# A graph transformer kernel: the last rows of x loaded first, six raw chunks in place of four at the start of layer 2, and three last chunks scaled one by one

## The chip, the cores and the metric

The kernel runs on one core of a Trainium2 chip, all in fp32. The time is the device time of one execution in microseconds (us), as the median of several runs. A profiled execution gives, beside its own time, the span from its first to its last instruction and a trace of every instruction.

## The reference

Two transformer convolutions over one graph, N = 6250 nodes with D = 128 features, E = 106,250 edges sorted by `dst`, H = 2 heads of C = 64; a batch norm and a relu between them; at the end the residual with x and a layer norm.

```python
def conv(h, edge_attr, src, dst, Wq, bq, Wk, bk, Wv, bv, We, Ws, bs):
    q, k, v = heads(h @ Wq + bq), heads(h @ Wk + bk), heads(h @ Wv + bv)
    e = heads(edge_attr @ We)                       # 96 attributes of an edge
    alpha = einsum('ehc,ehc->eh', q[dst], k[src] + e) / sqrt(C)
    ex = exp(alpha - segment_max(alpha, dst)[dst])
    a = ex / segment_sum(ex, dst)[dst]
    return segment_sum((v[src] + e) * a[:, :, None], dst) + h @ Ws + bs

edge_attr = concatenate([cos((node_vec[src] - t)[:, None] * time_w + time_b), msg])
h = conv(x, edge_attr, src, dst, ...)               # layer 1
h = relu((h - h.mean(0)) / sqrt(h.var(0) + 1e-5) * bn_g + bn_b)
h = conv(h, edge_attr, src, dst, ...)               # layer 2
return layernorm(x + h)
```

## The kernel before

**Tiles.** The edges are cut into NC = 106 chunks. A chunk has up to CE = 1024 edges (eight row tiles of 128) that end in up to NN = 64 nodes, 64 x 2 heads = 128 columns. Because `Wq` and `Wk` are multiplied together ahead of time, a node's query is a column of a *table*: `tables` makes 512 nodes' worth of it (a *block*, 13 of them) and writes it to DRAM, and a chunk loads its 64 nodes from there.

**A layer** is a call of `conv` (L699): one loop over rounds k (L964), in an order written out by hand (`manual_schedule`), so every engine gets its instructions in the order of the code. In round k:
- `fetch` and `gather` bring in chunk k+2 (layer 2) or k+4 (layer 1). `fetch` has SP issue the loads of the edge attributes, the table and, in layer 2, the stored time encoding, transposed attributes and residual. `gather` (L746) issues eight indirect DMAs on GpSimd, one per row tile of 128 source nodes. Each is made to wait for a step of TensorE (`behind`), so that the gathers of one chunk are spread over a round.
- TensorE scores chunk k (`score`, L840 and L841, in two halves), transposes the weights of chunk k-1 (`turn_weights`, L863), turns chunk k+1 (`turn_in`, L819), finishes chunk k-2 (`finish_turn`, `finish`), and sums the weighted rows of chunk k-1 (`gather_sums`, L871). The last sum's step releases the first gather of the next round.
- VectorE takes the minimum of the scores (`lowest`), divides the sums of chunk k-2 (`divide`, L878 to L881) and copies them for `finish` (L896). ScalarE takes the exponential (`weigh`, L853) and copies the turned tiles out of PSUM.
- `pull(extra, n)` (L1019) takes n steps of other work from a generator, `rest()`.

**What the layers read.** Layer 1 gathers from `xv_d`, a copy of x in DRAM with each node's time ahead of its row. At the start, SP loads x in four cuts of 12 row blocks (`load_features`, L502), then the last 106 rows that fill no whole block (`pl.rest`). `pass_features` (L520) copies the cuts beside the times, on VectorE and ScalarE in turns, and SP writes each to `xv_d`, the rest rows first of all. The code at L1338 to L1347 sets the order of these copies against the first table's matmuls and additions (`first_table`), and of `columns(flats[0], srcs)`, which makes the gathers' indices.

Layer 1 leaves its result h in SBUF, transposed (`hT`), 64 nodes per chunk; SP's DMA puts each there (L910). Layer 1's `rest()` (L1081) turns finished blocks of h back to rows and writes them to `h_d` in DRAM, each once `at_round[0]` has passed the last chunk that it needs by three; two of the blocks are left to round NC+1. At the end of layer 1 the batch norm's scale and shift are known, and layer 2 wants relu(scale*h + shift). The normalised rows go to a second array, `hn_d`, 13 blocks: `hide(n)` (L769) turns and writes n blocks (tile `fhn`, four buffers; VectorE's copy is L1065, SP's writes L1073 and L1078). Three are written in the run-up of layer 2, the others in rounds 0 and 1. Until they are there, chunks 0 to RAW-1 gather from `h_d`, raw; ScalarE then normalises the turned copy as it leaves PSUM (L821) and VectorE the rows themselves, for the sums (`normalise`, L886 and L887, three operations over 128x1024). Later chunks gather from `hn_d` and need neither.

Layer 2's `rest()` (L1175) makes block b of the table and of the residual x + h Ws in seven pulls, then two idle ones; a chunk can't be fetched before its block is written.

**The end.** `finish` of layer 2 collects centred rows in groups of up to ten chunks, which begin at the chunks in `STARTS` (L59). When a group's last chunk is in, ScalarE takes one square root for the group (L940), VectorE its reciprocal (L941), and each chunk's rows wait in `done` for `store` (L945): ScalarE scales them, SP writes them to the output. The last chunk's store is made up of two chunks' rows (`flast`, L954). All stores go through SP's queue.

Of the kernel before, what the change touches and what calls it, by code (L numbers as in the profile page):

```python
# [13 lines left out]
P = 128  # L14
# [33 lines left out]
NC = 106  # L48
# [7 lines left out]
HIGHEST = 2.0 ** 119  # L56

LG = 10
STARTS = (*range(0, 91, LG), 97, 102, 105)  # L59


@with_exitstack
# [439 lines left out]
def load_features(nc, pl, mw, x, node_vec):  # L502

    N = x.shape[0]
    NF = N // P
    NR = N - NF * P
    xall = pl.xall = pl.hT[:, :NF * D].rearrange("p (b d) -> p b d", d=D)
    pl.cuts = list(zip(range(0, NF, 12), [*range(12, NF, 12), NF]))
    for b0, b1 in pl.cuts:
        nc.sync.dma_start(xall[:, b0:b1], x[:NF * P, :].rearrange("(p b) d -> p b d", b=NF)[:, b0:b1])  # L510
        if b0 == 0:
            pl.times = mw.tile([P, NF], F32, name="fnv", bufs=1)
            nc.sync.dma_start(pl.times, node_vec[:NF * P].rearrange("(p b) -> p b", b=NF))
    if NR:
        nc.vector.memset(pl.rest, 0.0)
        nc.sync.dma_start(pl.rest[:NR, 1:], x[NF * P:N, :])
        nc.sync.dma_start(pl.rest[:NR, 0:1], node_vec[NF * P:N].rearrange("(p a) -> p a", a=1))


def pass_features(nc, pl, mw, dram, N):  # L520

    NF = pl.xall.shape[1]
    pl.xv_d = dram.tile([N, 1 + D], F32, name="xv_d")
    rows = mw.tile([P, NF, 1 + D], F32, name="fxrows", bufs=1)
    nc.vector.tensor_copy(rows[:, :, 0], pl.times)
    to = pl.xv_d[:NF * P, :].rearrange("(p b) d -> p b d", b=NF)
    if N > NF * P:
        nc.sync.dma_start(pl.xv_d[NF * P:N, :], pl.rest[:N - NF * P])
    for i, (b0, b1) in enumerate(pl.cuts):
        (nc.scalar.copy if i % 2 else nc.vector.tensor_copy)(rows[:, b0:b1, 1:], pl.xall[:, b0:b1])  # L530
        nc.sync.dma_start(to[:, b0:b1], rows[:, b0:b1])
        yield

# [127 lines left out]
def ordered(ctx: ExitStack, tc: tile.TileContext, pl, x, dst, edge_attr_64, conv2, bn_g, bn_b, out):  # L661


    nc = tc.nc
    N = x.shape[0]
# [9 lines left out]
    at_round = [0]  # L675
# [16 lines left out]

    SINGLE = 40

    RAW = 4

    hidden = list(range(-(-N // GE)))

    def conv(c, extra, first_blocks=None):  # L699
# [46 lines left out]
        def gather(k, rows, behind=None):  # L746
            f = ch[k].f
            for t in rows:
                row = nc.gpsimd.indirect_dma_start(  # L749
                    out=f[:, t, (1 if c else 0):1 + D], out_offset=None, in_=(h_d[:N, :] if k < RAW else hn_d) if c else pl.xv_d,  # L750
                    in_offset=bass.IndirectOffsetOnAxis(ap=pl.srcs[:, t, k:k + 1], axis=0))
# [6 lines left out]
        def lead(k):  # L758
            return 2 if c else AHEAD
# [9 lines left out]
        def hide(n):  # L769
            step = None  # L770
            for b0 in hidden[:n]:
                step = put_rows(hn_d, b0, *turned_rows(b0, small.tile([P, GE // P, P], F32, name="fhn", bufs=4)))
            del hidden[:n]
            return step
# [35 lines left out]
        def turn_in(k, u):  # L810
# [7 lines left out]
            for t in range(4):  # L818
                last = nc.tensor.transpose(px[:, t * P:(t + 1) * P], s.f[:, u * 4 + t, 1:1 + D], ident)  # L819
            if c and k < RAW:  # L820
                nc.scalar.activation(s.ft[:, u * GE:(u + 1) * GE], px, AF.Relu, bias=pl.shift, scale=pl.scale)  # L821
# [12 lines left out]
        def score(k, u):  # L834

            s = ch[k]
            if u == 0:
                s.ps = p_s.tile([P, CE], F32, name="fps")
            w = slice(u * GE, (u + 1) * GE)
            half = nc.tensor.matmul(s.ps[:, w], s.tab[:, :, 0], s.ft[:, w], start=True, stop=False)  # L840
            return half, nc.tensor.matmul(s.ps[:, w], s.tab[:EC, :, 1], s.et[:, w], start=False, stop=True)  # L841
# [33 lines left out]
        def divide(k):  # L875
            s = ch[k]
            inv = small.tile([P, 1], F32, name="finv")
            nc.vector.tensor_scalar(inv, s.pa[:, D + ED:], 1e-30, None, op0=OP.max)  # L878
            nc.vector.reciprocal(inv, inv)
            s.a = small.tile([P, D + EW], F32, name="fa")  # L880
            nc.vector.tensor_scalar(s.a, s.pa, inv, None, op0=OP.mult)  # L881
# [16 lines left out]
        def finish(k):  # L898
# [24 lines left out]

            k0 = max(i for i in STARTS if i <= k)
            g = k - k0
            n = next(i for i in (*STARTS, NC) if i > k) - k0
            if g == 0:
# [30 lines left out]
        def pull(gen, n):  # L958
            for _ in range(n):
                next(gen, None)  # L960

        with cs, tc.manual_schedule():
            ended = None
            for k in range(-lead(-NC), NC + 3):  # L964
                def on(j):
                    return 0 <= j < NC

                coming = [j for j in range(k + lead(k - 1), k + lead(k) + 1) if on(j)]
                filling = False

                def bring(rows, behind=None):
                    for j in coming:
                        gather(j, rows, behind)

                for j in coming:
                    fetch(j)
                if k == -lead(-NC):
                    yield_first(bring)
                elif k < -1:
                    bring(range(T))  # L980
                elif not filling:
                    bring(range(1), ended)
                step = score(k, 0)[1] if on(k) else hide(1) if c and k == -1 else None
                if k >= -1 and not filling:
                    bring((1,), step)
                step = turn_weights(k - 1) if on(k - 1) else hide(1) if c and k == -1 else None
                if k >= -1 and not filling:
                    bring((2,), step)
                place()
                if on(k - 2):  # L990
                    divide(k - 2)
                half, step = score(k, 1) if on(k) else (hide(1) if c and k == -1 else None, None)
                if k >= -1 and not filling:
                    bring((3,), half if c else step or half)
                    if c:
                        bring((4,), step)
                if on(k - 2):
                    finish_turn(k - 2)
                if on(k):
                    lowest(k)  # L1000
                step = turn_in(k + 1, 0) if on(k + 1) else None
                if k >= -1 and not c:
                    bring(range(5) if filling else (4,), step)
                if on(k):
                    weigh(k)
                step = turn_in(k + 1, 1) if on(k + 1) else None
                if k >= -1:
                    bring((5,), step)
                for j in (k + 2,) if k < SINGLE else (k + 2, k + 3) if k == SINGLE else (k + 3,):
                    if c == 0 and on(j):  # L1010
                        encode(j)
                        if j < SINGLE + 3:
                            sine()
                if k >= 0:
                    at_round[0] = k
                    if c and k < 2:
                        hide(5)
                    else:
                        pull(extra, 2 if k < 4 or k > 96 else 1)  # L1019
                if len(args) == 3 or args and k == NC - 4:  # L1020
                    sine()
                if on(k - 2):
                    finish(k - 2)
                if c and on(k):
                    if k < RAW:
                        normalise(k)
                    nc.vector.tensor_copy(ch[k].f[:, :, 1 + D:1 + D + TD], ch[k].z)
                for _ in range(min(len(done), 4 if k >= NC else 2 if k > NC - 12 else 1)):
                    store(*done.pop(0))
                *steps, ended = gather_sums(k - 1) if on(k - 1) else (None, None, None)  # L1030
                if k >= -1:
                    for t, step in zip((6, 7), steps):
                        bring((t,), step)
            at_round[0] = 2 * NC
            for _ in extra:
                pass
            for rows in done:
                store(*rows)
# [4 lines left out]
    with tc.tile_pool(name="fpw", bufs=2) as pw:  # L1043
# [131 lines left out]
        def rest():  # L1175
            for b0 in range(1, NT):
                yield from block(b0)
                yield
                yield

        conv(1, rest(), first_blocks)


@with_exitstack
def tile_gnn_resnorm(ctx: ExitStack, tc: tile.TileContext, x, src, dst, edge_attr_64, edge_weight, node_vec,
                     time_w, time_b, conv1, conv2, bn_g, bn_b, out):
    nc = tc.nc
    N = x.shape[0]
# [10 lines left out]
    with tc.tile_pool(name="plan", bufs=1) as pl, tc.tile_pool(name="planw", bufs=2) as mw, \  # L1199
# [66 lines left out]
        NR = -(-NC // 16) * 16  # L1266
# [39 lines left out]
        passed = pass_features(nc, got, mw, made, N)  # L1306
# [32 lines left out]
        first_table = tables(nc, got, 0, xT0, 0, mw, wide)  # L1339
        next(first_table)  # L1340
        next(first_table)
        next(passed)
        for _ in first_table:
            pass
        columns(flats[0], srcs)
        for _ in passed:
            pass  # L1347
        got.tw = broadcast(nc, keep, "ftw", time_w, TD)
        got.tb = broadcast(nc, keep, "ftb", time_b, TD)
        nc.sync.dma_start(got.wv[0], conv1["Wv"])  # L1350
# [55 lines left out]
```

## Time and profile before

| | us |
|---|---|
| median of three runs | 2306.39 (2305.79 to 2308.45) |
| the profiled execution | 2306.31 |
| its span | 2304.3 |
| start to the first gather of layer 1 | 39.25 |
| from there to the first gather of layer 2 | to 1184.96 |
| the last gather of layer 2 | 2267.0 |

The mean granted clock of TensorE in the profiled execution is 0.983 of full speed. Busy time by stretch of the span (us from its start):

| stretch | TensorE | VectorE | ScalarE | GpSimd | granted clock | DMA engines' mean busy share |
|---|---|---|---|---|---|---|
| 0 to 39 | 22.9 | 20.1 | 9.9 | 5.0 | 0.87 | 0.84 |
| 40 to 1178, layer 1 | 1119.1 | 786.3 | 733.4 | 816.9 | 0.99 | 0.62 |
| 1178 to 1256, change of layer | 58.3 | 38.9 | 30.2 | 46.1 | 0.87 | 0.79 |
| 1256 to 2268, layer 2 | 988.5 | 386.7 | 440.6 | 759.9 | 0.99 | 0.67 |
| 2268 to 2304 | 22.3 | 10.7 | 13.1 | 0 | 0.88 | 0.04 |

A line of a timeline gives the start, the length, the engine (PE is TensorE, PEld its weight load, DVE VectorE, ACT ScalarE, POOL GpSimd; SPq and ACTq are the DMAs that SyncE and ScalarE issue), the line of the code, the operation, and the tiles out<-in. In square brackets stands how long the engine was idle just before, and what released it. "issue" means that it waited for nothing that the profile shows. GpSimd's busy time is a rough measure, since about 0.3 us pass between any two of its gathers.

### The profile page before, as it was taken

How to read it: one execution, taken by the hardware profiler on the slowest of the kernel's cores; microseconds unless marked ns; L12 is line 12 of the kernel's file. 1: busy time of each engine (PE TensorE's matmuls, PEld its weight loads, DVE VectorE, ACT ScalarE, POOL GpSimd, SP SyncE). 2: the span in 40 equal slices, each digit the busy share in tenths (PEclk: the TensorE clock that was granted, in tenths of full speed). 3: DMA queues.
4: the chain of work that ended last, by engine and by line, in shares of the span. 5: the costliest groups of instructions: out<-in, count | busy, mean ns of one | idle time of the engine just before them, and what ended most of it. 6: DMA issues, size and time to landing. Idle time of an engine off the chain costs nothing.

```text
span 2304.3 us, 40495 instructions
## 1 busy us (share of the span) xinstructions
PE 2210.9 (96%) x11589; PEld 1707.9 (74%) x11589; DVE 1243.7 (54%) x3745; ACT 1227.9 (53%) x1951; POOL 1628.7 (71%) x1717
## 2 busy tenths in 40 slices
PE   5999999999999999999978999999999999999996
PEld 3687888778887888888856777777777776777775
DVE  5576767676676767777635333433334343343332
ACT  3677777776666665555643444444444444444443
POOL 3777777777777777777536777777777777777772
PEclk7899999999999999999989999999999999999998
DMA  7666666656666666666548656676676676666562
GB/s 231 167 179 171 173 190 178 187 143 180 187 176 179 160 191 172 179 179 168 146 121 219 172 153 181 184 183 174 170 190 184 173 188 165 178 180 162 152 168 51
DMA packets 431095, 396.64 MB, mean 172 GB/s; under 512 B 279682, under 2 KB 375167, under 8 KB 427535
## 3 DMA queue, kind: packets, MB, share of 16 engines
q1 hardware_dynamic: 357648, 239.69, 38.1%
q0 software_dynamic: 54656, 113.07, 20.5%
q10 hardware_dynamic: 18558, 41.20, 5.0%
q8 instruction: 95, 1.56, 0.3%
q14 instruction: 138, 1.12, 0.2%
HBM read 277.16 MB, written 113.14 MB: 169 GB/s over the span
## 4 chain that ended last, share of the span: by engine, by line
PE 67%; DMA 6%; POOL 2%; issue 2%; DVE 1%; SPq 0%; ACT 0%; POOLq 0%; DVEq 0%; ACTq 0%
PE fpa L871 22%; PE fps L840 11%; PE fps L841 11%; PE fpx L819 6%; PE fppt L863 6%; DMA ff<-hn_d,fsrcs 5%; PE fpg L627 3%; PE fpe L828 2%; POOL ff L749 2%; PE fpo L921 2%; PE fpo L922 1%; PE fpo L893 1%; PE fpo L894 1%; PE fpo L903 1%; PE fpo L904 1%
## 5 line engine op out<-in xcount | busy, mean ns | idle before, releaser
L749 POOL DMA_INDIRECT ff<-xv_d,fsrcs x848 | 817.7, 964 | 304.0 <-issue 100.0
L749 POOL DMA_INDIRECT ff<-hn_d,fsrcs x816 | 775.6, 950 | 265.4 <-issue 107.1
L871 PE MATMUL fpa<-ff,fpt 128*128 128x225 f32 x3392 | 693.3, 357 | 0.0
L871 PEld LDWEIGHTS fpa<-ff,fpt 128*128 128x128 f32 x3392 | 627.4, 190 | 11.2 <-issue 0.7
L864 ACT COPY fpt<-fppt 128x512 f32<-128x512 f32 x424 | 228.0, 590 | 472.2 <-PE fppt L863 467.4
L840 PE MATMUL fps<-fft,ftab 128*128 128x512 f32 x848 | 442.9, 604 | 0.6 <-ACT fs L853 0.6
L823 ACT COPY fft<-fpx 128x512 f32<-128x512 f32 x416 | 242.1, 582 | 365.3 <-PE fpx L819 365.2
L896 DVE COPY fat<-fpo 128x256 f32<-128x256 f32 x212 | 90.1, 425 | 586.0 <-PE fpo L894 556.3
L853 ACT ACTIVATE fs<-fps,fm 128x1024 f32<-128x1024 f32 x212 | 236.3, 1114 | 85.8 <-DVE fm L848 83.4
L819 PE MATMUL fpx<-fident,ff 128*128 128x128 f32 x1696 | 248.2, 276 | 34.6 <-DMA ff<-hn_d,fsrcs 26.3
L863 PEld LDWEIGHTS fppt<-fident,fs 128*128 128x128 f32 x1696 | 198.4, 141 | 104.7 <-issue 103.6
L846 DVE TENSOR_REDUCE flow<-fps 128x1 f32<-128x1024 f32 x212 | 257.5, 1214 | 10.0 <-PE fps L841 10.0
L819 PEld LDWEIGHTS fpx<-fident,ff 128*128 128x128 f32 x1696 | 197.9, 141 | 46.4 <-DMA ff<-hn_d,fsrcs 34.3
L841 PE MATMUL fps<-fxT,ftab 112*128 112x512 f32 x424 | 218.4, 596 | 2.1 <-DMA fxT<-et_d 2.1
L863 PE MATMUL fppt<-fident,fs 128*128 128x128 f32 x1696 | 220.0, 272 | 0.0
L841 PE MATMUL fps<-fet,ftab 112*128 112x512 f32 x424 | 217.9, 595 | 0.0
L840 PEld LDWEIGHTS fps<-fft,ftab 128*128 128x128 f32 x848 | 166.6, 226 | 3.8 <-issue 2.2
L841 PEld LDWEIGHTS fps<-fet,ftab 112*128 112x128 f32 x424 | 106.5, 251 | 76.0 <-issue 58.7
L841 PEld LDWEIGHTS fps<-fxT,ftab 112*128 112x128 f32 x424 | 83.9, 198 | 102.0 <-issue 94.9
L794 DVE SCALAR_TENSOR_TENSOR farg<-fturns,farg 128x256 f32<-128x256 f32 x318 | 135.4, 426 | 10.9
L878 DVE TENSOR_SCALAR finv<-fpa 128x1 f32<-128x1 f32 x212 | 33.5, 158 | 191.7 <-PE fpa L871 185.3
L828 PE MATMUL fpe<-fident,ff 128*112 128x128 f32 x848 | 129.1, 275 | 1.5 <-DVE ff L806 1.5
(216 smaller groups left out, 2348.6 us busy)
## 6 DMA issues: line engine op xcount, KB each, us to landing
ff<-in_edge_attr SPq DMA_DIRECT2D x212, 256.0 KB
et_d<-fet SPq DMA_DIRECT2D x106, 448.0 KB
fxT<-et_d SPq DMA_DIRECT2D x106, 448.0 KB
ftab<-tab_d SPq DMA_DIRECT2D x106, 192.0 KB
tab_d<-fo ACTq DMA_DIRECT2D x13, 1536.0 KB
ff<-xv_d,fsrcs POOLq DMA_INDIRECT x848
enc_d<-fzs SPq DMA_DIRECT2D x106, 128.0 KB
ftab<-tab_d SPq DMA_DIRECT2D x106, 128.0 KB
```

The source lines that it names most:

```text
L749: row = nc.gpsimd.indirect_dma_start(out=f[:, t, (1 if c else 0):1 + D], out_offset=None, in_=(h_d[:N, :] if k < RAW else hn_d) if c else ...
L794: nc.vector.scalar_tensor_tensor(arg, turn, -part, arg, op0=OP.mult, op1=OP.add)
L819: last = nc.tensor.transpose(px[:, t * P:(t + 1) * P], s.f[:, u * 4 + t, 1:1 + D], ident)
L823: nc.scalar.copy(s.ft[:, u * GE:(u + 1) * GE], px)
L828: last = nc.tensor.transpose(pe[:EC, t * P:(t + 1) * P], s.f[:, u * 4 + t, 1 + D:], ident)
L840: half = nc.tensor.matmul(s.ps[:, w], s.tab[:, :, 0], s.ft[:, w], start=True, stop=False)
L841: return half, nc.tensor.matmul(s.ps[:, w], s.tab[:EC, :, 1], s.et[:, w], start=False, stop=True)
L846: nc.vector.tensor_reduce(low, s.ps, AX.X, OP.min)
L853: nc.scalar.activation(s.s, s.ps, AF.Exp, bias=s.bias, scale=-1.0)
L863: last = nc.tensor.transpose(pp[:, t * P:(t + 1) * P], s.s[:, at:at + P], ident)
L864: nc.scalar.copy(s.pt[:, u * GE:(u + 1) * GE], pp)
L871: nc.tensor.matmul(s.pa, s.pt[:, t * P:(t + 1) * P], s.f[:, t, 1:1 + D + EW], start=t == 0, stop=t == T - 1)
```

## The change

It has seven parts, at three places of the program.

At the start, the rest rows of x and their times are loaded ahead of the four cuts (`load_features`); of the four copies into `fxrows` ScalarE makes only the second and VectorE the other three; and the fourth copy is issued between the first table's two VectorE additions, ahead of `columns`, instead of behind it.

At the change of layer, the two row blocks of h that are left for round NC+1 are pulled ahead of that round's `finish_turn`. In layer 2, chunks 4 and 5 gather raw rows too (`RAW` 6). The ten row blocks of `hn_d` that remain after the run-up are written four, three and three in rounds 0, 1 and 2, instead of five and five in rounds 0 and 1, and layer 2 pulls two steps of its other work per round in rounds 3 to 5 (before: rounds 2 and 3).

At the end, the groups that share a square root end at chunks 96, 100, 102, 103, 104 and 105, where before they ended at 96, 101, 104 and 105.

```diff
-STARTS = (*range(0, 91, LG), 97, 102, 105)
+STARTS = (*range(0, 91, LG), 97, 101, 103, 104, 105)
...
     pl.cuts = list(zip(range(0, NF, 12), [*range(12, NF, 12), NF]))
+    if NR:
+        nc.vector.memset(pl.rest, 0.0)
+        nc.sync.dma_start(pl.rest[:NR, 1:], x[NF * P:N, :])
+        nc.sync.dma_start(pl.rest[:NR, 0:1], node_vec[NF * P:N].rearrange("(p a) -> p a", a=1))
     for b0, b1 in pl.cuts:
...
-    if NR:
-        nc.vector.memset(pl.rest, 0.0)
-        nc.sync.dma_start(pl.rest[:NR, 1:], x[NF * P:N, :])
-        nc.sync.dma_start(pl.rest[:NR, 0:1], node_vec[NF * P:N].rearrange("(p a) -> p a", a=1))
...
-        (nc.scalar.copy if i % 2 else nc.vector.tensor_copy)(rows[:, b0:b1, 1:], pl.xall[:, b0:b1])
+        (nc.scalar.copy if i == 1 else nc.vector.tensor_copy)(rows[:, b0:b1, 1:], pl.xall[:, b0:b1])
...
-    RAW = 4
+    RAW = 6
...
                 if on(k - 2):
                     divide(k - 2)
+                if c == 0 and k == NC + 1:
+                    at_round[0] = k
+                    pull(extra, 2)
                 half, step = score(k, 1) if on(k) else (hide(1) if c and k == -1 else None, None)
...
                     at_round[0] = k
-                    if c and k < 2:
-                        hide(5)
+                    if c and hidden:
+                        hide(4 if k == 0 else 3)
                     else:
-                        pull(extra, 2 if k < 4 or k > 96 else 1)
+                        pull(extra, 2 if c and k < 6 else 2 if k < 4 or k > 96 else 1)
...
         next(first_table)
         next(first_table)
         next(passed)
+        next(first_table)
+        for _ in passed:
+            pass
         for _ in first_table:
             pass
         columns(flats[0], srcs)
-        for _ in passed:
-            pass
```

## The prediction

> **What bounds the kernel now.** Chunk *k* of a layer is one round: TensorE scores chunk *k*, turns chunk *k*+1, sums chunk *k*-1 and finishes chunk *k*-2, while GpSimd issues the eight row gathers of chunk *k*+2 in layer 2. I read the page first, then GpSimd's timeline around the change of layer, then the timelines of the start and of the end. The page's group of layer 2's gathers, and GpSimd's timeline (start us, length, what; in brackets the idle time before it and its releaser):
>
> ```profile
> L749 POOL DMA_INDIRECT ff<-hn_d,fsrcs x816 | 775.6, 950 | 265.4 <-issue 107.1
> ```
> ```profile
> 1225.07 0.95 POOL L749 DMA_INDIRECT ff<-h_d,fsrcs  x1 [0.30 <-issue]
> 1232.29 0.95 POOL L749 DMA_INDIRECT ff<-hn_d,fsrcs  x1 [6.27 <-DMA hn_d<-fhn]
> ...
> 1237.29 1.49 POOL L749 DMA_INDIRECT ff<-hn_d,fsrcs  x1 [0.30 <-issue]
> ...
> 1253.51 0.95 POOL L749 DMA_INDIRECT ff<-hn_d,fsrcs  x1 [3.46 <-PE fpa L871]
> 1254.76 0.95 POOL L749 DMA_INDIRECT ff<-hn_d,fsrcs  x1 [0.30 <-issue]
> 1256.01 0.95 POOL L749 DMA_INDIRECT ff<-hn_d,fsrcs  x1 [0.30 <-issue]
> ```
>
> A gather follows the last after 1.25 us (0.95 + 0.30), so eight make 10.0 us. TensorE's round takes 9.27 us alone (score starts 1274.80 and 1284.08), 10.13 with one table product (1304.92 to 1315.06), 10.17 with a residual (1255.36 to 1265.53): (4 x 10.13 + 10.17 + 2 x 9.27)/7 = 9.89 over a block's seven pulls. GpSimd's issue sets layer 2's pace by a hair, and from 1256.01 to the last gather (2267.0) it runs at 1.264 per gather. What GpSimd loses before 1256 is not regained: the stall of 6.27 at the first normalised row, and 3.46 soon after. TensorE and VectorE between these:
>
> ```profile
> 1227.53 0.29 DVE L1065 COPY fhn<-fpg 128x128 f32<-128x128 f32 x1 [3.93 <-DMA hn_d<-fhn]
> 1232.16 0.33 PE L893 MATMUL fpo<-fident,fa 128*128 128x128 f32 x1 [2.02 <-DVE fa L881]
> 1247.73 1.05 PE L819 MATMUL fpx<-fident,ff 128*128 128x128 f32 x2 [2.63 <-DMA ff<-hn_d,fsrcs]
> ```
>
> The 13th copy waits for a free `fhn` buffer, `normalise(1)` and `divide(0)` queue behind it on VectorE, and TensorE waits 2.02 for `fa`; then chunk 4's late rows hold TensorE until 1248.3. The start and the end:
>
> ```profile
> 2.99 0.36 SPq L510 DMA_DIRECT2D fhT<-in_x  x1
> 6.61 0.33 ACTq L551 DMA_DIRECT2D fbs<-in_L_gnn_bs  x1
> 19.72 0.96 DVE L530 COPY fxrows<-fhT 128x1536 f32<-128x1536 f32 x1
> 24.28 0.23 SPq L528 DMA_DIRECT2D xv_d<-fxrest  x1
> 33.66 0.29 DVE L1367 SCALAR_TENSOR_TENSOR fmoved<-apart,left,fmoved 128x64 f32<-128x64 f32 x1
> 38.62 0.06 DVE L689 MEMSET qpi<- 128x1 f32 x1 [4.67 <-DMA xv_d<-fxrows]
> 39.25 0.96 POOL L749 DMA_INDIRECT ff<-xv_d,fsrcs  x1 [27.80 <-DVE fbits L732]
> ```
> ```profile
> 2284.14 0.16 DVE L878 TENSOR_SCALAR finv<-fpa 128x1 f32<-128x1 f32 x1 [1.79 <-PE fpa L871]
> 2294.97 0.34 DVE L954 SCALAR_TENSOR_TENSOR flast<-fout,flate,fpg 64x128 f32<-64x128 f32 x1 [0.47 <-ACT fout L947]
> 2298.65 0.48 SPq L956 DMA_DIRECT2D out<-flast  x1
> ```
>
> At the start everything waits for the five `xv_d` writes, all held until 24.28 behind the last rows of x. At the end the last tile is ready at 2295.31 and issued 3.34 later, because SP's last stores go one after the other, each behind its predecessor's landing (up to 2.9).
>
> **The change, part by part.**
>
> *Start.* The rest rows go first, so the writes go out as the copies end, not at 24.28. The DMA shares of the 2 us windows from 2 to 38 add up to 32.5 us, so all transfers could have landed by about 34.5. Two things take part of that back. VectorE gets the fourth copy (0.96, L530's row) between the two table additions; ScalarE loses its own of 1.47 there, which held nothing. And in the built program x's first block now waits on the semaphore of ScalarE's 256 KB load of x, which freed L551 at 6.61, where it waited on a small one before (2.99): 0 to 3.6 later. Engines were at 0.92 and more from 2 to 22, so other loads fill part of it; I take 1.5, below the middle. The copy of block 0 moves by it, and ahead of the matrices' VectorE steps it moves them all. VectorE's end: 33.95 + 0.96 + 1.5 = 36.4, plus 0.7 for the branch (TensorE's: 32.43 to 33.13) = 37.1, plus the 0.63 from 38.62 to 39.25: first gather at 37.7, **gain 1.5**. Bounds: +3.0 with no slip, -0.6 with all of 3.6. GpSimd issues without a break from there to 80 us and TensorE waits for it, so the shift passes on.
>
> *Boundary of the layers.* The last two row blocks (five transposes, copies 0.89, three DMAs of 0.41 + 0.92) move ahead of `finish_turn(105)`. Their data is there (the `fhT` write of chunk 104 lands near 1175). On VectorE the copies stand before `fat`: 1176.42 + 0.89 + 0.42 = 1177.73 against 1177.43, a loss of 0.30. SP's store of `fres` went at 1179.79 behind them though `fres` was ready at 1178.79; now at 1179.15. **Gain 0.6**; bounds 0 and 1.0 (the whole wait on SP). L916's `h_d` row follows on the same queue, and the first gather (1184.96) comes 3.0 after its issue, as `hn_d`'s came 3.7 after.
>
> *Chunks 4 and 5 raw, row blocks over three rounds.* Removed: GpSimd's stall (6.27 - 0.30 = 5.97), the buffer wait 3.93 and the 1.27 before it in round 0 (three blocks in the run-up + 4 + 3 + 3 never want a buffer whose write is not long landed). Added: two `normalise` of 2.48 + 0.69 = 3.17 on VectorE, and 0.19 per ScalarE half (0.78 against 0.59). Moved: tables of block 1 from rounds 2 and 3 to rounds 3 and 4; from round 5 on the pulls have caught up (6 done in both), and chunk 8, the first to need them, is fetched in round 6. Round by round on TensorE, with the old clock: round 1 starts at 1213.5 but is held at `turn_in(2)` by its gathers until 1219 as before; 12 transposes instead of 17 and no buffer wait, sums end at 1223.9 (was 1225.5). Round 2: no wait for `fa`; `turn_in(3)` ends when its last gather (1225.07) has landed, about 5.5 later at this DMA load: 1231; 9 transposes, sums end 1235.9 (1239.0). GpSimd goes on at 1226.3 with chunk 4, held from its sixth row by `turn_in(3)`, last row at 1235.1, landed 1240.6. Round 3 (scores end 1240.3) then turns chunk 4 without the waits, sums end 1247.1 (1255.5). Chunk 6's first row would follow at 1247.1 against 1256.01: 8.9. GpSimd alone gives 1184.96 + 48 x 1.25 + 1.2 = 1246.2: 9.8, the upper bound. The DMA engines are the friction: shares of 0.9 to 1.19 from 1202 to 1247 but for 1229 to 1232 (0.28) and 0.27, 0.08 after it, some 7 us unused that the same bytes must now fill. I take **7.5**. Lower bound 3.4: only TensorE's waits on chunk 4's rows (0.62 + 2.63 and its loader's share) go. SP: the last `hn_d` write is issued about 1233.5, lands 3.7 later, 1237, 9 before chunk 6 asks; that slack is the cover. VectorE has 3.9 (usual) + 3.17 + 2.2 (two L633) = 9.3 in round 4 of 10.1, and the order puts `divide(3)` 0.6 ahead of TensorE's need: nothing exposed, but that cover is thin.
>
> [...] In the trace gathers beside L886 took 0.95 (1253.51, 1254.76), once 1.49: 0.54 at most per `normalise`, not 3.17. [...]
>
> *The tail.* Groups end at chunks 100, 102, 103, 104, 105. Only chunk 104's store stands before the last, so the 3.34 on SP goes. But in the built order of round 105 the load of Exp's table carries the wait for `fm(105)`: 2281.43 + 1.28, Exp to 2283.8, square 0.50, root's table 1.28, root to 2285.6, reciprocal 2285.8, L1027's copy 0.28, and only then `divide(104)`: 2286.1 against 2284.14, on the chain: 1.95 lost. `flast` at 2297.3, issued 2297.4 (chunk 104's store, 2291.2 + 2.9, is down). **Gain 1.3**; bounds +3.3 (the divide not held) and -0.7 (the tables loaded one by one twice on the chain, another 2.0).
>
> [...]
>
> Sum: 1.5 + 0.6 + 7.5 + 1.3 = 10.9 off the profiled execution's 2306.31 (span 2304.3 and 2.0 around it), itself 0.08 below the median: **2295.5**.
>
> **Rivals.**
> 1. *The stall changes owner.* GpSimd's rows are tied to TensorE's steps, and gathers on saturated DMA land late (6.65 for chunk 4's last), so only 3.4 comes: 2306.4 - 6.8 = 2299.6. For it: the 3.46 wait on L871. Against: that wait itself came from the late chunk 4. Chance 0.20.
> 2. *Everything pays.* 3.0 + 1.0 + 9.8 + 3.3 = 17.1: 2289.3. Against: the divide in the built order. Chance 0.10.
> 3. *Slower: VectorE bounds rounds 2 to 5.* If `normalise` waits on gathers at the head of VectorE's queue, `divide` and the minimum behind it come late, GpSimd, tied to TensorE, keeps losing its 6, and 2 x 3.17 + 2.3 (table additions) = 8.6 come on top: 2306.4 + 8.6 - 3.4 = 2311.6. It decides once VectorE is busy for the whole of rounds 4 and 5. Against: 9.3 of 10.1. Chance 0.05.
> 4. *It doesn't do what it says:* the start's slip is full, the rows come as late: -0.6 + 0.6 + 3.4 - 0.7, 2303.7. Chance 0.05.
>
> My forecast has 0.60. Together 2289.5 to 2302.5 holds 8 in 10. A difference under 0.2% (4.6 us) this kernel's measurement can't tell from none: faster 0.87 (forecast, rivals 1 and 2, less a little), within 0.2% 0.08, slower 0.05.
>
> **What would show it.** First gather near 37.7 (39.25); SP's `fhT` store of chunk 105 0.6 sooner after its sums; no wait on `hn_d` in GpSimd's queue, chunk 6's first row about 71 after the layer's first gather less 7.5; TensorE's wait for `fa` gone in round 2; SP issuing the last store at once, but `divide(104)` 2 late. Wrong: a wait on `hn_d` at chunk 6, `fa` waits in rounds 4 to 6, or a first gather after 39.

## The result, and the profile after

| | before | changed |
|---|---|---|
| median of 8 runs each, us | 2306.56 (2303.14 to 2310.41) | 2298.89 (2291.86 to 2300.53) |
| profiled execution, us | 2306.31 | 2300.53 |
| its span, mean granted clock | 2304.3, 0.983 | 2298.7, 0.986 |

The medians differ by 7.7 us. The ratio of the runs is 0.9964, with a 95% interval of 0.9951 to 0.9976: 8.3 us faster (5.5 to 11.3), where 10.9 were predicted. The profiled execution of the changed kernel is the slowest of its eight, so its stretches add up to less (5.5) than the medians' difference.

Stretches of the two profiled executions, each between the starts of two instructions, but for `flast`'s end (worked out from the timelines):

| stretch | before | changed | gained | predicted |
|---|---|---|---|---|
| start to the first gather | 39.25 | 40.01 | -0.76 | 1.5 |
| to `divide(105)` of layer 1 (L879) | 1136.52 | 1137.68 | -1.16 | 0 |
| to the first gather of layer 2 | 9.19 | 8.24 | 0.95 | 0.6 |
| to the first gather of chunk 6 | 71.05 | 63.86 | 7.19 | 7.5 |
| to the last gather of layer 2 | 1010.07 | 1014.15 | -4.08 | 0 |
| to the end of `flast` | 29.23 | 29.17 | 0.06 | -1.95 |
| to the issue of its store | 3.34 | 0.03 | 3.31 | 3.24 |

The page's group of layer 2's gathers from `hn_d` in the changed kernel (sixteen fewer, which are raw now):

```profile
L749 POOL DMA_INDIRECT ff<-hn_d,fsrcs x800 | 759.2, 949 | 256.2 <-issue 105.5
```

Its mean tells nothing of the change; the timeline does. The change of layer, in GpSimd's timeline of the changed kernel:

```profile
1246.51 1.70 POOL L749 DMA_INDIRECT ff<-h_d,fsrcs  x1 [0.30 <-PE fpa L871]
1248.51 0.98 POOL L749 DMA_INDIRECT ff<-h_d,fsrcs  x1 [0.30 <-PE fpa L871]
1249.79 0.94 POOL L749 DMA_INDIRECT ff<-hn_d,fsrcs  x1 [0.30 <-issue]
```

and VectorE's beside it:

```profile
1246.16 2.48 DVE L886 TENSOR_TENSOR ff<-ff,fspread 128x1024 f32<-128x1024 f32 x2
1248.67 0.69 DVE L887 TENSOR_SCALAR ff<-ff 128x1024 f32<-128x1024 f32 x1
```

The wait on `hn_d` is gone: chunk 6's first row starts 0.30 after the gather before it. But the gather issued while L886 runs took 1.70 instead of 0.95. Each of the six calls of `normalise` has such a gather beside it (1.33 to 1.71), and the first residual's two additions have one of 1.42. Over the first 80 gathers of layer 2 the length beyond 0.945 (their *surplus*, from lengths printed to 0.01) adds up to 4.12, and to 0.87 before.

The loss of 4.08 in the long stretch is a loss of GpSimd's lead, not of TensorE's. TensorE's lead on the kernel before is 4.05 where VectorE takes the minimum of chunk 10's scores (1316.10 against 1320.15) and 4.12 at chunk 102's copy `fat` (2266.29 against 2270.41). GpSimd was 2.2 further ahead at chunk 6 than TensorE could use (6.22). In between the lead moves from 5.6 (chunk 54) to -1.8 (chunk 96) and back, with waits of 0.5 to 2.8 for single late rows. So what the change of layer was worth is read at chunk 10's minimum: 135.19 after layer 2's first gather before, 130.17 now, 5.0.

The start, and then the end, in the timelines of the changed kernel:

```profile
2.95 0.24 SPq L511 DMA_DIRECT2D fxrest<-in_x  x1
6.88 0.37 SPq L514 DMA_DIRECT2D fhT<-in_x  x1
13.56 0.21 DVE L525 COPY fxrows<-fnv 128x48 f32<-128x48 f32 x1 [4.00 <-DMA fnv<-in_node_vec]
30.91 0.36 ACTq L637 DMA_DIRECT2D tab_d<-fo  x1
37.85 0.28 DVE L1371 SCALAR_TENSOR_TENSOR fmoved<-apart,left,fmoved 128x64 f32<-128x64 f32 x1
39.38 0.06 DVE L689 MEMSET qpi<- 128x1 f32 x1 [1.25 <-DMA tab_d<-fo]
40.01 0.96 POOL L749 DMA_INDIRECT ff<-xv_d,fsrcs  x1 [29.09 <-DVE fbits L732]
```
```profile
2280.11 1.28 ACT L940 ACT_TABLE_LOAD   x1
2281.64 0.15 DVE L941 RECIPROCAL fvar<-fvar 64x1 f32<-64x1 f32 x1 [1.37 <-ACT fvar L940]
2281.91 0.14 DVE L878 TENSOR_SCALAR finv<-fpa 128x1 f32<-128x1 f32 x1
2282.88 0.30 PE L893 MATMUL fpo<-fident,fa 128*128 128x128 f32 x1 [1.93 <-DVE fa L881]
...
2292.77 0.34 DVE L954 SCALAR_TENSOR_TENSOR flast<-fout,flate,fpg 64x128 f32<-64x128 f32 x1 [0.47 <-ACT fout L947]
2293.14 0.48 SPq L956 DMA_DIRECT2D out<-flast  x1
```

The first cut of x leaves at 6.88 (2.99 before), so the copy of the times waits until 13.56 (9.62 before) and the whole chain is late. What the first gather waits for at last is no longer `xv_d` but the store of the first table, issued at 30.91 (26.72 before). At the end TensorE idles 1.93 for `fa`, because `divide(104)` stands behind the root of chunk 103's group, so that from chunk 103's `fat` to `flast`'s end 17.54 pass (15.62 before); the last store goes at once.

The experiments ran on different chips. On two of them the kernel before itself takes 2686 to 2691 us, so totals are compared with the kernel before on the same chip, and stretches among runs of chips with the same total (the start alone, whose operations take the same time on both kinds, is once compared across them).

### The profile page after: what moved, and what is told of

It is laid out like the page before. It is cut to its first block, busy times and chain, and to the rows that moved or that the text cites. A ratio compares the mean times of both kernels' runs of the same rounds, so it can differ in the third digit from the quotient of the medians.

```text
span 2298.7 us, 40506 instructions
## 1 busy us (share of the span) xinstructions
PE 2208.5 (96%) x11589; PEld 1708.4 (74%) x11589; DVE 1247.3 (54%) x3756; ACT 1230.0 (54%) x1954; POOL 1628.1 (71%) x1717
## 3 DMA queue, kind: packets, MB, share of 16 engines
q1 hardware_dynamic: 357648, 239.69, 38.4%
## 4 chain that ended last, share of the span: by engine, by line
PE 68%; DMA 6%; POOL 2%; issue 2%; DVE 1%; ACT 0%; POOLq 0%; SPq 0%; ACTq 0%
PE fpa L871 22%; PE fps L840 11%; PE fps L841 11%; PE fpx L819 6%; PE fppt L863 6%; DMA ff<-hn_d,fsrcs 4%; PE fpg L627 3%; PE fpe L828 2%; POOL ff L749 2%; PE fpo L921 2%; PE fpo L922 1%; DMA ff<-h_d,fsrcs 1%; PE fpo L893 1%; PE fpo L894 1%; PE fpo L903 1%
## 5 line engine op out<-in xcount | busy, mean ns | idle before, releaser
L749 POOL DMA_INDIRECT ff<-hn_d,fsrcs x800 | 759.2, 949 | 256.2 <-issue 105.5
L794 DVE SCALAR_TENSOR_TENSOR farg<-fturns,farg 128x256 f32<-128x256 f32 x318 | 135.4, 426 | 10.9
```

The lines of the kernel that those rows point to most:

```text
L749: row = nc.gpsimd.indirect_dma_start(out=f[:, t, (1 if c else 0):1 + D], out_offset=None, in_=(h_d[:N, :] if k < RAW else hn_d) if c else ...
L794: nc.vector.scalar_tensor_tensor(arg, turn, -part, arg, op0=OP.mult, op1=OP.add)
```

## The experiments

### Each part alone

The kernel before with one part of the diff each; all four on one chip (the kernel before: 2690.53).

```diff
 start_alone: the hunks of load_features, pass_features and the copies' order
+        nc.sync.dma_start(pl.rest[:NR, 1:], x[NF * P:N, :])       # ahead of the cuts
...
 boundary_alone
+                if c == 0 and k == NC + 1:
+                    at_round[0] = k
+                    pull(extra, 2)
 raw_spread_alone: the hunks of RAW, hide and pull
+    RAW = 6
+                        hide(4 if k == 0 else 3)
 tail_alone
+STARTS = (*range(0, 91, LG), 97, 101, 103, 104, 105)
```

> The kernel before with the start's part alone (rest rows of x first, the copies' engines and order). Theory (the first cut of x waits for the semaphore of ScalarE's large load, so VectorE's whole chain of the start moves by some 4 us): SP issues the first cut near 6.9, VectorE's last operation of the start ends near 38.1, first gather at 40.0 (before 39.25); what follows in layer 1 moves by between -1.0 and +0.8, so the total is 0 to 1 away from before. Rival (in the changed kernel the first gather was late by chance or through the other parts): first gather at 37.7, total 1.5 lower.

> The kernel before with the two row blocks pulled ahead of finish_turn(105) alone. Theory: from VectorE's divide(105) of layer 1 to the first gather of layer 2 8.44 (before 9.38), total 0.9 lower; layer 1 up to that divide as before. Rival (the blocks ahead of the divide cost VectorE what they give SP): 9.4 and no change.

> The kernel before with six raw chunks, row blocks over three rounds and two pulls in rounds 3 to 5 alone. Theory (GpSimd's stalls go, but with them the cover under which normalise and the pulls ran: gathers beside normalise take 1.4 to 1.7, and TensorE's rounds 4 and 5 take 11.0 and 10.2): layer 2's first gather to chunk 6's first 63.9 (before 71.05), to chunk 8's first 85.7 (before 91.5), chunk 8's minimum 5 earlier against the first gather, total 5 lower. Rival (the shortfall in the changed kernel was this one execution's late rows): chunk 8's first gather after 84 or less and the total 7.5 lower.

> The kernel before with the new groups alone. Theory: last store issued 0.03 after flast (before 3.34), divide(104) comes 1.9 later against chunk 103's copy fat than before, total 1.4 lower. Rival (the divide is not held, the extra tables are hidden): total 3.3 lower. Rival 2 (TensorE's last rounds absorb both): no change.

| run | ratio, interval | start to first gather | `divide(105)` to layer 2 | to chunk 6 / 8 | minimum of chunk 10 | `fat(103)` to `flast` | `flast` to its store |
|---|---|---|---|---|---|---|---|
| start_alone | 0.9998, 0.9983 to 1.0012 | 37.03 | 9.14 | 76.28 / 102.33 | 154.66 | 15.61 | 3.43 |
| boundary_alone | 1.0003, 0.9990 to 1.0017 | 40.42 | 8.24 | 75.59 / 99.37 | 151.20 | 15.62 | 3.35 |
| raw_spread_alone | 0.9971, 0.9954 to 0.9987 | 38.70 | 9.16 | 70.74 / 94.07 | 144.33 | 15.62 | 3.71 |
| tail_alone | 1.0006, 0.9992 to 1.0019 | 39.55 | 9.13 | 77.76 / 102.00 | 153.55 | 17.56 | 0.02 |

Three of the effects are plain in the stretches. The boundary gives 0.9 (8.24 against 9.13 to 9.16), as the theory had it. The tail delays `flast` by 1.94 and saves 3.3 to 3.7 at its store. The raw rows and the spread are the only part whose total moves: 0.0029 of 2690.53 is 7.8 us (3.5 to 12.4). Chunk 6's first row comes 5.8 earlier than the mean of the other three (76.54), chunk 10's minimum 8.8 earlier than theirs (153.14). The interval holds both the theory's 5 and the rival's 7.5, so it doesn't decide between them. The totals of the other three are too coarse for effects of 1 to 2.5 us.

The start came out as the rival had it: 37.03, not 40.0. The first cut went at 5.97, the times were copied at 11.59 instead of 13.56, and no landing held the first gather. So the 40.01 of the first profile isn't the part's fixed cost; how late the first cut goes varies, and with it everything behind.

### The changed kernel again, and its start and tail redone

```diff
 better: the changed kernel, with
+            if NR:                       # behind the first cut and the times
+                nc.sync.dma_start(pl.rest[:NR, 1:], x[NF * P:N, :])
...
-STARTS = (*range(0, 91, LG), 97, 101, 103, 104, 105)
+STARTS = (*range(0, 91, LG), 97, 101, 103, 105)
```

> The changed kernel once more, as the yardstick of this chip. Theory (the start's chain hangs on the landing of the times, which the first cut's wait holds back, and that landing varies by some us): VectorE's copy of the times between 11.5 and 13.6, first gather 25.4 to 26.5 after it, between 37 and 40; divide(105) of layer 1 to layer 2's first gather 8.24; layer 2's first gather to chunk 6's 63.9 and to chunk 8's 85.7; chunk 103's fat to flast 17.55. Rival (these stretches are one execution's accident): they move by 1 or more against the first profile.

> The changed kernel with two parts redone: the rest rows of x are loaded behind the first cut and the times (ahead of the other three cuts), and the groups end at chunks 100, 102, 104 and 105. Theory: the first cut goes out near 3.0 and the times are copied near 10, VectorE's start ends near 35.2 and the first gather comes at 36.0 to 36.5; chunk 103's fat to divide(104) 4.65 instead of 6.5, the last store waits 0.5 behind two others instead of 0.03: fat(103) to its issue 16.1 (changed kernel 17.6). Together 3 to 4 below the changed kernel. Rival (the transfers themselves set the start): first gather no earlier than in after_again, held by a landing of xv_d or tab_d, and only the tail's 1.4.

On their chip the kernel before takes 2306.25. The changed kernel has 2298.77, ratio 0.9963 (0.9953 to 0.9974): the first result again. 'better' has 2292.61, ratio 0.9949 (0.9931 to 0.9966).

Of the changed kernel's stretches, the start (first gather 38.25, 25.85 after the copy of the times) and the boundary (8.15) came as expected. Two did not. Chunk 6's first gather came 67.52 after layer 2's first, chunk 8's 89.40, chunk 10's minimum 133.73: TensorE waited 1.06 and 2.12 for late rows of chunk 3, and GpSimd 2.96 for TensorE. So this stretch varied by 3.7 between these two executions, and this profile too is the slowest of its series (2304.55, where the median of ten is 2298.77). And from `fat(103)` to `flast` took 19.23, not 17.55. In after_again, TensorE's timeline, and then three stretches of the span (each line has start and end; length; busy time and count of PE, PEld, DVE, ACT, POOL; granted clock; DMA share; GB/s):

```profile
2285.16 0.30 PE L893 MATMUL fpo<-fident,fa 128*128 128x128 f32 x1 [1.93 <-DVE fa L881]
...
2286.71 4.99 PE L871 MATMUL fpa<-ff,fpt 128*128 128x225 f32 x16
```
```profile
2279.00:2283.00 4.00, 4.00 (x25) 3.75 (x24) 1.34 (x7) 3.30 (x5) 0.00 (x0) 1.00 0.01 4
2283.00:2287.00 4.00, 1.55 (x14) 1.05 (x12) 1.64 (x7) 2.22 (x5) 0.00 (x0) 0.99 0.03 8
2287.00:2292.00 5.00, 4.70 (x16) 4.00 (x15) 1.06 (x8) 1.01 (x4) 0.00 (x0) 0.67 0.02 7
```

The sixteen matmuls of the last sums took 4.99; in the first profile, after the same wait of 1.93, they took 3.31. The granted clock is 0.67 where they run. The same loss (19.23) is in hide5_raw6 below, and not in no_normalise (17.55) nor in tail_alone (17.56): two of the five executions with this wait. The wait for `divide(104)` can cost its 1.9 and 1.7 more.

In 'better', the tail went as worked out: `fat(103)` to `divide(104)` 4.64, to `flast` 15.62, and its store 0.43 later, together 1.5 under the changed kernel's 17.57. The start went half way:

```profile
2.96 0.36 SPq L510 DMA_DIRECT2D fhT<-in_x  x1
9.89 0.21 DVE L525 COPY fxrows<-fnv 128x48 f32<-128x48 f32 x1 [0.29 <-DMA fnv<-in_node_vec]
27.46 0.36 ACTq L637 DMA_DIRECT2D tab_d<-fo  x1
34.06 0.28 DVE L1371 SCALAR_TENSOR_TENSOR fmoved<-apart,left,fmoved 128x64 f32<-128x64 f32 x1
36.56 0.06 DVE L689 MEMSET qpi<- 128x1 f32 x1 [2.21 <-DMA tab_d<-fo]
37.19 0.96 POOL L749 DMA_INDIRECT ff<-xv_d,fsrcs  x1 [26.07 <-DVE fbits L732]
```

With the first cut out at 2.96 again, VectorE is done at 34.34, 3.8 before the changed kernel's first profile. But the table's store, 9.1 from issue to landing, now holds the first gather for 2.21. The theory's first half is shown, and the rival's landing is what comes next. Nor was the new place of the rest rows free: the second cut of x now left at 9.39 (8.40 in the changed kernel, 6.81 before), and ScalarE's copy waited 2.61 for it.

### What holds GpSimd at the change of layer

```diff
 no_normalise: the changed kernel without normalise, so that raw rows go into the sums
-                    if k < RAW:
-                        normalise(k)
 hide5_raw6: the changed kernel with
-                    if c and hidden:
-                        hide(4 if k == 0 else 3)
+                    if c and k < 2:
+                        hide(5)
...
+                        pull(extra, 2 if k < 4 or k > 96 else 1)
```

> The changed kernel without VectorE's normalise of the six raw chunks (their raw rows go into the sums; scores stay as they are). Theory (a gather that is issued while L886 runs ends late, and GpSimd has no stall left to hide it in): of the first 80 gathers of layer 2 the length beyond 0.945 adds up to under 1 (4.1 in the changed kernel), layer 2's first gather to chunk 6's 61.0 (63.9), to chunk 8's 82.7 (85.7), total 2 to 3 lower. Rival (TensorE's rounds with two pulls set the pace there): gathers are short again, but chunk 8's minimum comes no earlier against the first gather, total unchanged.

> The changed kernel with row blocks again five and five in rounds 0 and 1 and two pulls in rounds 2 and 3, so that of this part RAW 6 alone is left. Theory (most of the gain is that GpSimd has raw rows to gather while hn_d is written; the spread only takes away the wait for a free fhn buffer): layer 2's first gather to chunk 6's 64 to 66, chunk 8's 86 to 88, VectorE waits again for a buffer at the 13th copy. Rival (the spread carries half of it): chunk 6's at 68 or later, TensorE waits for fa in round 2 by 2 as before.

| run | median, ratio | surplus of 80 gathers | first gather of chunk 6 / 8 | minimum of chunk 4 / 8 / 10 |
|---|---|---|---|---|
| before, first profile | 2306.56 | 0.87 | 71.05 / 91.50 | 75.48 / 114.91 / 135.19 |
| changed, first profile | 2298.89, 0.9964 | 4.12 | 63.86 / 85.73 | 67.47 / 109.89 / 130.17 |
| after_again | 2298.77, 0.9963 | 3.53 | 67.52 / 89.40 | 71.14 / 113.46 / 133.73 |
| better (this part unchanged) | 2292.61, 0.9949 | 2.57 | 63.64 / 84.31 | 67.25 / 107.84 / 128.11 |
| no_normalise | 2295.39, 0.9963 | -0.07 | 60.45 / 81.31 | 64.50 / 105.08 / 125.36 |
| hide5_raw6 | 2300.11, 0.9968 | 1.46 | 66.06 / 86.60 | 70.49 / 110.11 / 130.38 |

(All but the medians in us from layer 2's first gather.) Without normalise no gather is long, and every mark comes 2.7 to 3.2 before the fastest run of this table that has it. The marks are as the theory had them, not the rival. But this is one execution, the fastest of its seven, and among the others the same marks differ by up to 5.6, so how much of the lead is normalise's isn't shown. The total fell by 3.4, which its interval (0.9948 to 0.9977) doesn't separate from the changed kernel.

RAW 6 alone gives nearly all, as far as one profile each can tell: hide5_raw6 lies between the two profiles of the changed kernel at every mark, and its median is 1.3 above. VectorE's wait before the 13th copy is back (3.10, at 1226.44; the trace puts its end down to a step of TensorE that ended then, so that the buffer holds it again is inferred), and TensorE waits 1.19 for `fa` (2.02 before). The last column shows why the spread brings so little. From chunk 4's minimum to chunk 8's the kernel before takes 39.4 and hide5_raw6 39.6; with the pulls moved to rounds 3 to 5 it is 40.6 to 42.4. Rounds 4 and 5 together then hold two table products and a residual, where they held a residual alone: two products of 0.86 more (10.13 against 9.27), 1.7 together, where the stretch grew by 1.2 to 3.0, at a time when TensorE has no wait left to put them in.

### The spread of the kernel before, and normalise from PSUM

```diff
 better2: 'better', with
-        next(first_table)
         for _ in passed:
             pass
-        for _ in first_table:
-            pass
         columns(flats[0], srcs)       # the two loops in the other order
 better3: 'better2', with
+        both = p_a.tile([P, GE], F32, name="fpa")
+        sums, wide = both[:, :D + EW], both[:, 2 * P:].rearrange("p (i d) -> p i d", d=D)
+        if c:
+            nc.vector.tensor_copy(wide, pl.spread)
...
-                nc.vector.tensor_tensor(rows, rows, pl.spread[:, None, i].to_broadcast([P, T, D]), op)
+                nc.vector.tensor_tensor(rows, rows, wide[:, None, i].to_broadcast([P, T, D]), op)
 better4: 'better3', with normalise(k) moved behind gather_sums(k - 1) of its round
```

> The kernel before once more, for the spread of its stretches. Theory (the stretches are the kernel's, not one execution's): first gather between 38.5 and 40, divide(105) of layer 1 to layer 2's first gather 9.2, layer 2's first gather to chunk 6's 71 and to chunk 8's 91.5 within 2, chunk 103's fat to flast 15.6 and the last store 3.3 behind flast. Rival: the first profile was an odd one, chunk 6's comes at 68 or before, and part of the gain read from it was chance.

> The kernel of 'better' with the fourth copy behind both table additions (still on VectorE, still ahead of the indices). Theory (the first gather waits for the landing of the first table's store, issued 9 us before): the store is issued 0.9 sooner against the copy of the times, first gather near 36.3 (37.2 in 'better'); the rest as in 'better'. Total 0 to 1 below 'better', 6 to 7 below the changed kernel's 2298.8. Rival (the landing is set by the amount moved, not by when the store is issued): first gather 37.2 as before.

> The kernel of 'better2' with normalise reading the batch norm's scale and shift from PSUM (in the half of the sums' bank that is free), so that L886 reads one operand from SBUF instead of two. Theory (GpSimd's gather is held while VectorE reads two operands from SBUF): no gather beside normalise takes over 1.0, the first 80 gathers' surplus falls from 2.6 to 4.1 to under 0.5, chunk 6's first gather 60.5 to 61 after layer 2's first, chunk 8's 81 to 82, total 3 below 'better2'. Rival (any long VectorE operation that writes SBUF holds the gather, or the one at L887 does): gathers of 1.3 to 1.7 stay, chunk 6's at 63.5 or later, no change.

> The kernel of 'better3' (scale and shift read from PSUM) with normalise(k) behind the sums of chunk k-1 in VectorE's order, since in 'better3' the sums waited for it (they share its PSUM tile). Theory: no gather of the first 80 is stretched (surplus under 0.5), no wait of the sums for normalise, divide(k-1) comes 3.2 later and is still in time by 0.4; layer 2's first gather to chunk 6's 3 less than in the changed kernel (60.5 to 61 on a chip like the first, 68 to 69 on the slower one where 'better2' had 71.9), total 2 to 4 below 'better2'. Rival (the late divide is exposed): TensorE waits for fa 1 or more in several of rounds 2 to 7 and nothing is gained on 'better2'.

before_again, better2 and better3 ran on a chip where the kernel before has 2686.34. before_again (one run, 2687.16): first gather 40.11, boundary 9.04, chunk 6 after 75.69, chunk 8 after 99.45, `fat(103)` to `flast` 15.62 and 3.68 to its store. Against the three runs above that leave the change of layer as it was (75.59 to 77.76, 99.37 to 102.33), its 71.05 on the first chip couldn't be tested; the other stretches hold within 1.

better2: 2677.04, ratio 0.9966 (0.9944 to 0.9987); first gather 37.38, again behind the table's store, by 2.03. The third copy itself waited 2.49 for its cut, so where the fourth stands could not show. That question is open.

better3: 2702.77, ratio 1.0074 (1.0049 to 1.0099), slower. The gathers are short: surplus -0.19, and one gather of 1.09 is the longest. But the sums now wait for normalise, since both use the one PSUM tile:

```profile
1413.98 5.65 PE L876 MATMUL fpa<-ff,fpt 128*128 128x225 f32 x16 [6.28 <-DVE ff L891]
1432.31 5.03 PE L876 MATMUL fpa<-ff,fpt 128*128 128x225 f32 x16 [5.66 <-DVE ff L891]
```

(L876 is the sums' line there, L891 normalise's.) The gain was handed over to a new wait, with the matmuls behind it at 5.0 and more instead of 3.3.

better4, on a chip where the kernel before has 2307.39: 2292.66, ratio 0.9940 (0.9920 to 0.9961). Surplus 0.57, and no gather that is issued in the pair at L891 is long:

```profile
1233.00 2.48 DVE L891 TENSOR_TENSOR ff<-ff,fpa 128x1024 f32<-128x1024 f32 x2 [2.01 <-PE fpa L876]
1233.04 0.94 POOL L749 DMA_INDIRECT ff<-h_d,fsrcs  x1 [0.30 <-DMA hn_d<-fhn]
1234.29 0.94 POOL L749 DMA_INDIRECT ff<-h_d,fsrcs  x1 [0.30 <-issue]
```

Most of the surplus is in two gathers (1.24 at 1215.02, 1.19 at 1224.05), and each was issued while the third operation of `normalise` ran (L892, which reads its one tensor from SBUF). So the pair isn't the only operation beside which a gather is late, and that part of better3's rival holds.

TensorE never waits for `fa` there. Chunk 6 comes after 62.04, chunk 8 after 83.67, 1.6 and 0.6 before 'better', chunk 10's minimum at 128.02 as in 'better' (128.11). GpSimd's time is free, and now TensorE's steps, to which the gathers are tied, hold it (waits of 0.5 to 1.2). So short gathers brought 1.6 at chunk 6 and nothing on TensorE in this one execution, and 1.6 is less than executions of one kernel differ; through what else no_normalise may gain its 2.7 there stays open. 'better' and better4 can't be told apart by their intervals. Both lie clear below the kernel before: by 0.0051 and 0.0060 of 2306 to 2307, 11.8 and 13.8 us. Their medians lie 6 us below the changed kernel's, but the intervals overlap with its (0.9953 to 0.9974), so that gain isn't separated from noise.

## Why the prediction was right, and where it was not

The forecast's direction held, all four parts gained, the change of layer most of all, and the time lies in its range. Two terms, the start and the change of layer, were too large, and two stretches held costs that the forecast didn't foresee.

**Start: 1.5 predicted, 0.55 to 1.2 measured.** The changed kernel's start ran in four profiles on chips of the usual total: first gather at 40.01, 38.25, 38.40 and 38.14, mean 38.70, against 39.25 in the one of before, a gain of 0.55. That one execution is a thin yardstick: the old start came at 38.70, 39.55, 40.11 and 40.42 on the other chips, the new one at 37.03, and over all five profiles of each the means are 39.6 and 38.4, a gain of 1.2. (From the copy of the times to VectorE's last operation the old start takes 24.1 to 24.6 on both kinds of chip.) VectorE's end was predicted at 36.4; it came at 38.13, 36.27, 35.79 and 36.33, mean 36.6. The slip of the first cut was larger than the 1.5 taken: it left at 5.94 to 6.88, which is 3.0 to 3.9 late, at the top of the range given (0 to 3.6) and beyond it, and the times were copied 2.3 to 3.9 late. The chain behind them was shorter than worked out, which made up for it. What failed is the next step, "plus 0.7 for the branch": VectorE's end no longer set it. The first table's store had moved with the chain, and its landing held the first gather 1.2 to 2.0 beyond VectorE's end. The prediction named the `xv_d` writes as what everything waits for, and didn't ask what is late next. By `divide(105)` nothing is left of the 0.55, against the same one execution: 1174.49 to 1177.69, mean 1176.0, against 1175.77. With the cut first again ('better', better4) it comes at 1174.01 and 1174.31.

**Boundary: 0.6 predicted, 0.9 measured** (9.04 to 9.19 in five runs without it, 8.15 to 8.31 with it). The wait on SP was the mechanism, and nearly the whole of its bound of 1.0.

**Change of layer: 7.5 predicted; 7.2 at chunk 6 in the first profile, 5.0 at chunk 10's minimum.** Three executions gave 7.2, 3.5 and 7.4 at chunk 6, and 5.0, 1.5 and 7.1 at the minimum. The stall on `hn_d`, the wait for `fhn` and the wait for `fa` went as worked out. Two prices failed. `normalise` was read from three gathers as 0.54 at most for each of the two new ones. What a gather loses depends on when it is issued, counted from the start of the pair of operations at L886. The one at 1237.29, 0.56 after that start, lost 0.54; of the two that were read as unharmed one (1253.51) had been issued 0.05 before its pair and the other (1254.76) 1.20 after its pair's start. In the changed kernel's first profile all six pairs, not only the two new ones, met a gather 0.33 to 0.71 after their start, and it lost 0.4 to 0.8. In hide5_raw6 five of the six met theirs after 0.7 to 1.1, and the surplus is 1.46. In the three runs with this part unchanged it is 2.6 to 4.1, against 0.87 before. And the moved pulls were given no price: the lead on chunk 4's minimum was 8.0 in the first profile, and rounds 5 to 8 gave 3.0 of it back. What was said of VectorE holds: in rounds 2 to 8 of the changed kernel TensorE never waited for `fa` in three profiles.

Beside L886's pair, which reads both operands from SBUF, a gather issued 0.33 to 0.71 after its start was late (1.33 to 1.71 in the changed kernel's first profile); beside the pair with one operand in PSUM it took 0.94 (better4). Of the pair's 2.48 a gather lost 0.8 at most, and nothing where its own 0.95 ended late enough (1254.76 to 1255.71 in the kernel before, beside a pair that ended at 1256.04).

**Tail: 1.3 predicted, 1.4 measured in the first profile** (3.31 saved at the store, 1.86 lost at `divide(104)`: 6.51 from `fat(103)` against 4.65), the loss being worked out as 1.95. What was not foreseen is the clock: in two of five executions the wait cost 1.69 more.

Rival 1 (gathers tied to TensorE, rows late, 2299.6) is what the second profile's change of layer shows, and the median, 2298.89, lies between it and the forecast's 2295.5, nearer to the rival. So the total in its range doesn't vouch for the terms: the moved pulls and the clock were in none of them, and normalise was priced too low. Sum of the means: 0.55 + 0.95 + 4.5 + (1.45 - 0.85) = 6.6, or 7.3 with 1.2 for the start, where the medians differ by 7.7; the rest is within what the long stretch of layer 2 adds or takes from one execution to the next (966.6 to 972.4 from chunk 10 to the last gather).

## What to carry to other kernels

Where the cost of one engine's operation to another depends on when they meet, price it as a rule of that time and not from the few meetings that the old kernel happens to hold: here three of them read as 0 to 0.54, and in the first profile of the changed kernel all six fell where 0.4 to 0.8 is lost. When a wait is taken away, list everything that moved with the chain that fed it, and ask which of these lands last; here the first table's store took the place of the rows. Before putting a load first on a queue, look at what semaphore its successor will wait for: the rest rows first made the first cut 3 to 4 us late, and put second they left it at 2.96, at the expense of the second cut.

## What the runs showed of the hardware

- TensorE's clock fell after an idle time of only 1.93 us (with one of 0.52 soon after it): sixteen matmuls took 4.99 in two executions, at a granted 0.67 (after_again, 2287 to 2292), and 3.31 at 1.00 in three others, after the same wait. In the first profiles of both kernels the granted clock is 0.5 or 1.0, and any two of its changes lie 3.413 us or a multiple of it apart (at 0.5 from 2125.77 to 2129.18 and from 2166.73 to 2173.56 in the changed kernel's). In the 3.41 before the fall TensorE was busy for 1.26 (after_again, 2283.52 to 2286.93) and 1.09 (hide5_raw6, 2278.52 to 2281.93). In the changed kernel's first profile it was busy for 1.58 from 2279.37 to 2282.78 and the clock stayed at 1.00; elsewhere in that profile the clock fell after such a stretch with 1.70 (2122.35 to 2125.77) and one with 1.59 (2163.32 to 2166.73). So TensorE's busy time in that stretch doesn't by itself tell when the clock falls, and what does isn't shown.
- In the traces a gather issued during the pair of operations at L886 ended no sooner than 0.43 to 0.45 before the pair did, whenever it was issued (first profile: 1217.49, 1225.51, 1237.43, 1248.21, 1260.04 and 1270.07 against 1217.93, 1225.95, 1237.87, 1248.64, 1260.48 and 1270.51). So one that was issued u after the pair's start lost 2.48 - 0.44 - 0.945 - u, about 1.1 - u; in the eleven profiles with that pair this fits all 37 gathers with u under 1.1 to 0.02. One that was issued 0.05 before the pair (1253.51 in the kernel before) took its usual 0.95.
- Chips differ: where the kernel before takes 2687.16, VectorE's copy `fat` starts over 1 us after TensorE's transposes (L894) have ended in 98 of 212 rounds, in the first profile in none. What holds it there is not seen in the trace.
